# Four chunks of x in two loads, and one weight-block sum ordered behind four evictions, in a two-layer kernel with an order planned ahead

## The chip, the cores and the metric

The kernel runs on one core of a Trainium2 chip. The metric is the time of one execution on the device, in microseconds (us), of which the median of the runs is given.

## The reference, cut to what matters

There are 8 batches of 256 rows of x with 1024 features each, all in float32. Two layers follow each other, each with a residual. The first one's weights are a fixed matrix plus a sign matrix of the batch's own (an integer mask of zeros and ones), scaled by the batch's coefficient. The second one's weights are one of 8 matrices, chosen by the batch's index.

```python
output = jnp.einsum('bsi,oi->bso', hidden_states, W) + b
sign = (2 * mask - 1).astype(hidden_states.dtype)
diff = jnp.einsum('bsi,bio->bso', hidden_states, sign)
return output + diff * coeff[:, None, None]
...
w = weight[adapter_ids]
return jnp.einsum('bsi,boi->bso', x, w)
...
x = x + _L0_cond_ref(x, L0_cond_W, L0_cond_b, condB_coeff, mask_Bx4096x4096_ik1)
x = x + _L1_cond_ref(x, L1_cond_weight, itok_B_3_7)
```

## The kernel before, in words

**Stages.** There are 16 stages, (layer, batch): (0,0), (1,0), (0,1), (0,2), (1,1), (0,3), (1,2) and so on to (1,7) (L233). The first stage is made alone, in plain matmuls; each other stage is one product of x (256 rows) with a weight matrix of 1024 by 1024, cut in blocks of two by two ("11", "12", "21", "22"), and made by Strassen's scheme in Winograd's form: seven half-size products p1 to p7 in place of eight (L22), in the order p1, p5, p6, p2, p7, p3, p4 (L31). Each product is 16 matmuls in float32, each of which stands as two records in the profile.

**The first stage.** Its contraction of 1024 is made in 8 chunks of 128 rows. For chunks 0 to 2 the loads of a chunk's mask and weights come in two halves, for chunks 3 to 7 in one piece, so that there are 11 pieces, numbered n = 0 to 10; pieces 7, 8, 9 and 10 are the chunks 4, 5, 6 and 7. For each piece the mask comes by DMA, ScalarE turns it into a scaled sign (L307), VectorE adds the weights w0T ("fold", L315) and TensorE multiplies (L322). Mask and weights go out on SyncE's DMA queue (SP) in turns, the mask first but for piece 0 (L280 to L295). x of the first batch, transposed, goes out on the same queue between them (L275): chunk 0 behind the mask of piece 0, chunk 1 behind the weights of piece 1, chunks 2 and 3 behind the weights of piece 3, and chunks 4 to 7 together (x0d, 512 KB) behind the mask of piece 7. The last two chunks are multiplied in halves of the output: chunk 6 and chunk 7 of the first half, then both of the second half (L390). Four evictions add x and the bias and write the result, transposed, for the next stage: L349, two after the first half of the output, two after the second. They are the tasks collected in yT[0][1], which the second stage knows as `got`.

**The second stage**, (1,0), takes that transposed result with the operands of the matmul exchanged ("flipped", L602). Its weight blocks come as w1T by DMA, in the order 11, 12, 22, 21 (L528). VectorE makes the sums of weight blocks t1 = 12 - 11 (in two halves in this stage), t2 = 22 - t1, t3 = 22 - 12 and t4 = 21 - t2 (L568), and the sums of x blocks s1 to s4 (L551). p1 needs block 11 and the first two evictions; p5 needs s1 and t1, and s1 needs all four evictions; p6 needs s2 and t2; p7 needs s3 and t3; p4 needs t4. The products gather in three PSUM banks; copies by ScalarE (L653) and additions by VectorE (L681) read them out between products, and the next product into a bank waits for that.

**The stages after.** For layer 0 the mask blocks come by DMA (L515), ScalarE scales them (L524) and VectorE folds the weights in (L538). x comes as rows (xR, L417) and transposed (xT, L492), and the bias is added by a DMA of GpSimd's queue (L427). A result of layer 0 is turned for layer 1 by transposes on VectorE (L448) and 32 moves on ScalarE (L462).

**What sets the order.** A planner (L83) simulates all tasks with fixed lengths (a product 3.435, a block sum or fold 2.21, a small VectorE operation 0.61, a load 2.50 apart and 2.2 to land; L47) and writes each engine's order out, which is then the program's order[...]. Of the tasks that are ready, an engine takes the one with the earliest due time (`latest`), which is counted back from a timetable of the products: the second stage begins at 34.5, and each product is 3.435 after the one before. Blocks of weights, loaded or summed, stand in 11 buffers; t1 (of the second stage), t2 and t3 take a fresh one. A load waits for its buffer on the SP queue, and all loads behind it wait too.

In the second stage the three sums are asked for in these lines; the list in brackets says what they wait for besides their operands:

```python
if s == 1:
    sum_of("t1")
    sum_of("t2", got)
    sum_of("t3")
else:
    sum_of("t3")
    sum_of("t1", [done["t3"]])
    sum_of("t2")
```

Of the kernel before, what the change touches and what calls it, by code (L numbers as in the profile page):

```python
# [14 lines left out]
P = 128  # L15
# [127 lines left out]
def kernel(  # L143
# [9 lines left out]
    x0b: bass.AP,  # L153
    x0c: bass.AP,
    x0d: bass.AP,
    mask0: bass.AP,
    bias: bass.AP,
    biasT: bass.AP,
# [64 lines left out]
    def task(*args, **kw):  # L223
        tasks.append(Task(*args, **kw))
        return tasks[-1]

    def take(r: Buffer):
        count[0] += 1
        r.tile = pools[r.pool].tile(shapes[r.pool], F32, tag=r.pool, name=f"{r.pool}_{count[0]}")
        return r.tile  # L230
# [28 lines left out]
    x0 = Buffer("a")  # L259
# [11 lines left out]
    def m_view(k: int):  # L271
        flat = m[k // 2].tile.rearrange("p k n -> p (k n)")
        return flat.rearrange("p (k n) -> p k n", k=2)[:, k % 2]

    def load_x0(lo: int, source):  # L275
        size = source.shape[1] - PAD
        flat = x0.tile.rearrange("p q k n -> p (q k n)")
        nc.sync.dma_start(out=flat[:, ds(lo * 2 * TH, size)], in_=source[:, 0:size])  # L278

    def load_first(n: int, what: str):  # L280
        k, cols = pieces[n]
        if what == "mask":
            if m[k // 2].tile is None:
                take(m[k // 2])
            nc.sync.dma_start(out=m_view(k)[:, cols].bitcast(I32), in_=mask0[k][:, cols])  # L285
        elif n == 0:
            nc.sync.dma_start(out=w0_sb[:, 0 : B + cols.size], in_=w0T[0][:, 0 : B + cols.size])  # L287
        else:
            nc.sync.dma_start(
                out=w0_rows[:, k, cols], in_=w0T[k][:, ds(B + cols.start, cols.size)]  # L290
            )
        if what == "w" and n in (1, 3):
            load_x0(*{1: (1, x0b), 3: (2, x0c)}[n])
        if what == "mask" and n in (0, 7):
            load_x0(*{0: (0, x0a), 7: (4, x0d)}[n])  # L295

    def parts(n: int):

# [60 lines left out]
    for n, (k, cols) in enumerate(pieces):  # L359
        share = cols.size / D  # L360
        opens = opened != k // 2
        length = {0: 0.4, 6: 0.75}.get(n, 1.22 * share)

        loads_ = {}
        for what in ("w", "mask") if n == 0 else ("mask", "w"):
            takes = [m[k // 2]] if opens and what == "mask" else []
            loads_[what] = task(
                "DMA",
                1.32 * share,
                lambda n=n, what=what: load_first(n, what),  # L370
                takes=takes,
                uses=[] if takes or what == "w" else [m[k // 2]],
                latency=1.5,
                latest=0.2 * n + 0.1 * len(loads_),
            )
        ld, ld2 = loads_["mask"], loads_["w"]
        sc = task("ACT", length, lambda n=n: scale_first(n), after=[ld], uses=[m[k // 2]])
        fo = task("DVE", length, lambda n=n: fold_first(n), after=[sc, ld2], uses=[m[k // 2]])
        folded.append(fo)
        last_scale = sc  # L380
        opened = k // 2
        if n == 0:
            first_w = ld2
            ld.takes = [x0, *ld.takes]
            ld.uses = [x0, *ld.uses]
            x0.users += 1
# [91 lines left out]
    def stage(s: int):  # L478
# [7 lines left out]
        if layer == 0:  # L486
            A = Buffer("a")
            got = [
                task(
                    "DMA",  # L490
                    LOAD,
                    lambda: nc.sync.dma_start(out=take(A)[:, 0:4], in_=xT[b - 1]),  # L492
                    takes=[A],
                    latency=LATENCY,
                    earliest=begin - 7 * PRODUCT,
                )
            ]
        else:
            A, got = yT[b]
# [4 lines left out]
        def part(name: str):  # L504
            if flipped and name == "s3":
                return (apart.tile if apart.tile is not None else take(apart))[:, 0].rearrange(
                    "p (k n) -> p k n", k=KH
                )
            return A.tile[:, A_SLOT[name]]
# [35 lines left out]
        def sum_of(what: str, after=()):  # L545
            left, op, right = SUMS[what]
            if what[0] == "s":
                done[what] = task(
                    "DVE",
                    SMALL,  # L550
                    lambda: v.tensor_tensor(part(what), part(left), part(right), op),  # L551
                    after=[*got, done.get(left), done.get(right), *after],
                    takes=[apart] if flipped and what == "s3" else [],
                    uses=[A],
                )
                return
            src = [W[left], W[right]]
            fresh = what in ("t2", "t3") or (what == "t1" and s == 1)
            W[what] = Buffer("w") if fresh else W[left]

            parts = (slice(0, KH),)
            if s == 1 and what == "t1":
                parts = (slice(0, KH // 2), slice(KH // 2, KH))

            def emit(rows):
                a, c = src[0].tile[:, rows], src[1].tile[:, rows]
                to = W[what].tile if W[what].tile is not None else take(W[what])
                v.tensor_tensor(to[:, rows], a, c, op)  # L568

            for n, rows in enumerate(parts):  # L570
                t = task(
                    "DVE",
                    BLOCK / len(parts),
                    lambda rows=rows: emit(rows),
                    after=[done[left], done[right], done.get(what), *after],
                    takes=[W[what]] if fresh and n == 0 else [],
                    uses=src + ([W[what]] if fresh and n else []),
                )
                if fresh and n == 0:
                    t.stage = s  # L580
                done[what] = t
# [3 lines left out]
        if s == 1:  # L585
            sum_of("t1")
            sum_of("t2", got)
            sum_of("t3")
        else:
            sum_of("t3")  # L590
            sum_of("t1", [done["t3"]])
            sum_of("t2")
# [208 lines left out]
    for s in range(1, len(stages)):  # L801
        stage(s)
# [87 lines left out]
```

## Time and profile before

| what | value |
|---|---|
| median of 3 runs | 403.43 us (403.40 to 403.67) |
| the profiled execution's own time | 403.51 us |
| its span, first to last instruction | 401.8 us |
| TensorE busy (matmul) | 395.2 us |
| VectorE busy | 331.0 us |
| ScalarE busy | 184.4 us |
| granted TensorE clock | 1.000 |
| moved by DMA | 103.00 MB |

The profile names TensorE's matmuls PE, its weight loads PEld, VectorE DVE, ScalarE ACT, GpSimd POOL and SyncE's queue SP. A line of the timeline reads: start, duration (both in us), engine, source line, operation, written tile, read tiles, shapes, number of instructions merged in it, and in brackets the idle time of the engine ahead of it and what ended that. A line of the chain reads: start, duration, what. The row of digits for an engine or for DMA gives its busy share, in tenths, in each of 40 equal slices of the span (here of some 10 us each).

### The profile page before, as it was taken

What the parts mean: (1) busy time and instruction counts of PE and PEld (TensorE: products, weight loads), DVE (VectorE), ACT (ScalarE), POOL (GpSimd) and SP (SyncE); (2) the same over time, 40 slices, a digit from 0 to 9 for tenths busy, and PEclk for the clock granted to TensorE, in tenths of its full rate; (3) what the DMA queues carried; (4) which work ended last, traced back from release to release, by engine and by line L of the source; (5) the groups of instructions that cost most, each with busy time, mean ns of one, the idle gap of its engine ahead of it and who ended that gap; (6) DMA issues with size and microseconds to landing.
All of it is one profiled execution on the core that took longest, in us unless ns stands there. A gap on an engine that the chain in (4) does not pass through costs nothing.

```text
span 401.8 us, 3439 instructions
## 1 busy us (share of the span) xinstructions
PE 395.2 (98%) x1155; PEld 200.6 (50%) x1155; DVE 331.0 (82%) x307; ACT 184.4 (46%) x305; POOL 27.2 (7%) x44
## 2 busy tenths in 40 slices
PE   8999999999999999999999999999999999999996
PEld 4878995444444444444444444444444444444443
DVE  2347999999999999799968998789977999668142
ACT  4452635205952396880069600894109920291000
POOL 0100111100011100011010100101001020001101
PEclk9999999999999999999999999999999999999999
DMA  7999999993696829958399583997749694611102
GB/s 261 406 413 423 420 341 394 370 320 107 254 346 194 354 104 343 335 161 325 106 407 301 185 333 107 377 263 261 262 188 347 198 359 164 263 51 52 54 0 105
DMA packets 19154, 103.00 MB, mean 256 GB/s; under 512 B 2304, under 2 KB 2816, under 8 KB 9664
## 3 DMA queue, kind: packets, MB, share of 16 engines
q1 hardware_dynamic: 14544, 87.24, 56.3%
q0 software_dynamic: 4448, 15.47, 14.3%
q8 instruction: 9, 0.15, 0.1%
q10 hardware_dynamic: 144, 0.07, 0.1%
q14 instruction: 9, 0.07, 0.0%
HBM read 94.38 MB, written 8.39 MB: 256 GB/s over the span
## 4 chain that ended last, share of the span: by engine, by line
PE 89%; DMA 8%; issue 1%; DVE 1%; SPq 0%; DVEq 0%
PE ps L617 84%; PE ps L607 5%; DMA w<-w1T 4%; DMA w_sb<-w0T 2%; DMA w<-mask 2%; DVE a L349 0%; SPq L285 0%; DVE a L551 0%; SPq L278 0%; SPq L287 0%; DVE r L766 0%; DVE w L568 0%; DVEq L349 0%
## 5 line engine op out<-in xcount | busy, mean ns | idle before, releaser
L617 PE MATMUL ps<-w,a 128*128 128x512 f32 (+1 forms) x792 | 336.7, 588 | 0.0
L617 PEld LDWEIGHTS ps<-w,a 128*128 128x128 f32 x792 | 149.9, 190 | 186.7 <-issue 183.4
L568 DVE TENSOR_TENSOR w<-w,w 128x2048 f32<-128x2048 f32 (+1 forms) x61 | 136.9, 2252 | 3.8 <-PE ps L617 2.5
L462 ACT ACTIVATE a<-turn 32x256 f32<-32x256 f32 x224 | 92.8, 414 | 68.5 <-DVE turn L448 65.6
L681 DVE TENSOR_TENSOR r<-r,ps 128x512 f32<-128x512 f32 x73 | 49.0, 679 | 24.9 <-PE ps L617 24.6
L538 DVE TENSOR_TENSOR w<-w,w_sb 128x2048 f32<-128x2048 f32 x28 | 63.9, 2284 | 5.7 <-ACT w L524 5.7
L524 ACT ACTIVATE w<-w,cn_sb,c_sb 128x2048 f32<-128x2048 int32 x28 | 58.5, 2091 | 17.0 <-DMA w<-mask 16.7
L551 DVE TENSOR_TENSOR a<-a 128x512 f32<-128x512 f32 x59 | 39.4, 684 | 0.3
L653 ACT ACTIVATE s<-ps 128x512 f32<-128x512 f32 x15 | 8.9, 591 | 61.3 <-PE ps L617 53.9
L322 PE MATMUL ps<-a,w 128*128 128x256 f32 x128 | 28.9, 384 | 1.1 <-DVE w L315 1.1
L707 POOL DMA_DIRECT2D out<-r x31 | 17.0, 550 | 190.5 <-DVE r L681 190.4
L322 PEld LDWEIGHTS ps<-a,w 128*128 128x128 f32 x128 | 24.0, 192 | 6.1 <-DVE w L315 2.7
L653 ACT ACTIVATE u<-ps 128x512 f32<-128x512 f32 x15 | 8.9, 594 | 38.9 <-PE ps L617 38.8
L315 DVE TENSOR_TENSOR w<-w,w_sb 128x512 f32<-128x512 f32 (+2 forms) x13 | 10.5, 815 | 15.6 <-ACT w L307 8.7
L607 PE MATMUL ps<-a,w 128*128 128x128 f32 x192 | 22.0, 276 | 1.2 <-DVE a L551 1.2
L607 PEld LDWEIGHTS ps<-a,w 128*128 128x128 f32 x192 | 21.8, 192 | 1.5 <-DVE a L551 1.4
L448 DVE STREAM_TRANSPOSE turn<-r 128x512 f32<-128x512 f32 x28 | 19.7, 707 | 0.6
L427 POOL DMA_DIRECT2D r<-bias x7 | 8.7, 1245 | 169.1 <-DMA r<-xR 169.1
L307 ACT ACTIVATE w<-w,cn_sb,c_sb 128x512 f32<-128x512 int32 (+2 forms) x13 | 11.6, 909 | 14.7 <-DMA w<-mask 14.7
L681 DVE TENSOR_TENSOR r<-r,s 128x512 f32<-128x512 f32 x14 | 9.6, 684 | 6.6 <-ACT s L653 6.6
L681 DVE TENSOR_TENSOR r<-r,u 128x512 f32<-128x512 f32 x14 | 9.6, 685 | 3.4 <-ACT u L653 3.4
L812 PE MATMUL idle<-zeros 128*128 128x512 bf16 (+1 forms) x11 | 4.4, 593 | 1.2 <-DVE warm L807 1.2
(24 smaller groups left out, 23.1 us busy)
## 6 DMA issues: line engine op xcount, KB each, us to landing
w<-w1T SPq DMA_DIRECT2D x32, 1024.0 KB, 9.1
w<-mask SPq DMA_DIRECT2D x28, 1024.0 KB, 9.6
out<-r POOLq DMA_DIRECT2D x31, 256.0 KB, 7.3
r<-xR SPq DMA_DIRECT2D x7, 1024.0 KB, 6.8
a<-xT SPq DMA_DIRECT2D x7, 1024.0 KB, 6.9
r<-bias POOLq DMA_DIRECT2D x7, 1024.0 KB, 15.8
w<-mask SPq DMA_DIRECT2D x5, 512.0 KB, 9.1
w_sb<-w0T SPq DMA_DIRECT2D x5, 512.0 KB, 9.7
```

What stands on the lines that cost most here:

```text
L322: nc.tensor.matmul(out=t.rearrange("p (c n) -> p c n", c=half)[:, c % half], lhsT=m_view(k)[:, ts(oc, P)], rhs=x0_view()[:, k], start=k == ...
L448: lambda t=t, opens=not turned: v.transpose(out=(take(r) if opens else r.tile)[:, t], in_=view(source.tile)[:, 2 * t + j]),
L462: nc.scalar.activation(to[:, :, :, f], src[:, :, :, g], AF.Copy)
L524: nc.scalar.activation(t, t.bitcast(I32), AF.Identity, bias=cn_sb[:, b : b + 1], scale=c2_sb[:, b : b + 1])
L538: lambda q=q: v.tensor_tensor(W[q].tile, W[q].tile, w0[q], ALU.add),
L551: lambda: v.tensor_tensor(part(what), part(left), part(right), op),
L568: v.tensor_tensor(to[:, rows], a, c, op)
L607: nc.tensor.matmul(out=t[:, ts(c, TH)], lhsT=W[w].tile[:, k, ts(c, P)], rhs=part(a)[:, k], start=opens and c == 0 and k == 0, stop=k == KH ...
L617: nc.tensor.matmul(out=t[:, cols], lhsT=part(a)[:, k], rhs=W[w].tile[:, k, cols], start=opens and k == 0, stop=k == KH - 1, skip_group_che ...
L653: lambda: nc.scalar.activation(take(r), bank.tile, AF.Copy),
L681: v.tensor_tensor(to, left, get(r), op)
L707: lambda: (queue or nc.gpsimd).dma_start(out=out0[:, block(q)] if flipped else out[b - 1, :, int(q[0]) - 1, lo:hi], in_=R[b].tile[:, block ...
```

## The change

The loads of x for the first batch: x0d now holds chunks 4 and 5 alone (256 KB) and stays behind the mask of piece 7; a new array x0e holds chunks 6 and 7 (256 KB) and goes out behind the mask of piece 9, which is chunk 6. In the second stage, t3 gets the four evictions of the first stage as predecessors, as t2 had already. The rest of the diff passes the new array on. The lengths and the due times that the planner works with are not changed.

```diff
-        if what == "mask" and n in (0, 7):
-            load_x0(*{0: (0, x0a), 7: (4, x0d)}[n])
+        if what == "mask" and n in (0, 7, 9):
+            load_x0(*{0: (0, x0a), 7: (4, x0d), 9: (6, x0e)}[n])
...
         if s == 1:
             sum_of("t1")
             sum_of("t2", got)
-            sum_of("t3")
+            sum_of("t3", got)
...
-    for k, chunks in (("x0a", x0[:, 0]), ("x0b", x0[:, 1]), ("x0c", x0[:, 2:4]), ("x0d", x0[:, 4:8])):
-        arrays[k] = chunks.reshape(P, -1)
+    for k, lo, hi in (("x0a", 0, 1), ("x0b", 1, 2), ("x0c", 2, 4), ("x0d", 4, 6), ("x0e", 6, 8)):
+        arrays[k] = x0[:, lo:hi].reshape(P, -1)
...
-    for k in ("x0a", "x0b", "x0c", "x0d", "w0T", "mask0"):
+    for k in ("x0a", "x0b", "x0c", "x0d", "x0e", "w0T", "mask0"):
```

More of the change, by code (lines that the diff above doesn't have):

```diff
@@ L155 @@
     x0d: bass.AP,
+    x0e: bass.AP,
     mask0: bass.AP,
```

## The prediction

> **What bounds the kernel now.** I read the page's busy line first, then the chain that ended last, then the timelines of the stretch that the change touches.
>
> ```profile
> PE 395.2 (98%) x1155; PEld 200.6 (50%) x1155; DVE 331.0 (82%) x307; ACT 184.4 (46%) x305; POOL 27.2 (7%) x44
> DMA 7999999993696829958399583997749694611102
> PE 89%; DMA 8%; issue 1%; DVE 1%; SPq 0%; DVEq 0%
> ```
>
> TensorE is the bound nearly throughout; the DMA engines are full for the first nine slices (90 us). The 8% of DMA on the chain lie at its start, as the chain in order of time shows:
>
> ```profile
> 12.43 9.09 DMA w<-mask
> 21.54 14.64 DMA w<-w1T
> 36.20 0.03 DVE w L568
> ...
> 38.41 1.29 DVE a L349 x2
> 39.70 0.02 issue
> 39.73 0.70 DVE a L551
> 40.43 0.04 issue
> 40.48 21.70 PE ps L607 x192
> 62.18 336.52 PE ps L617 x792
> ```
>
> From 40.48 us on TensorE never stops. So whatever starts that row earlier is the kernel's gain, as long as no operand comes late afterwards. Ahead of it, the chain passes through a weight block landing at 36.18, a block sum (L568), two evictions and s1. The timelines of TensorE and VectorE show the stalls:
>
> ```profile
> 20.34 1.23 DVE L315 TENSOR_TENSOR w<-w,w_sb 128x1024 f32<-128x1024 f32 x1 [2.56 <-DMA w_sb<-w0T]
> 21.61 14.08 PE L322 MATMUL ps<-a,w 128*128 128x256 f32 x64 [0.66 <-DVE w L315]
> 28.82 1.23 DVE L315 TENSOR_TENSOR w<-w,w_sb 128x1024 f32<-128x1024 f32 x1 [2.13 <-ACT w L307]
> 33.78 4.71 DVE L568 TENSOR_TENSOR w<-w,w 128x1024 f32<-128x1024 f32 x3 [0.74 <-DMA w<-w1T]
> 38.41 1.28 DVE L349 TENSOR_TENSOR a<-ps,r 128x512 f32<-128x512 f32 x2
> 40.48 10.98 PE L607 MATMUL ps<-a,w 128*128 128x128 f32 x96 [1.21 <-DVE a L551]
> ```
>
> Two stalls concern us. At 20.95 TensorE waits 0.66 us for chunk 4's fold, itself waiting for chunk 4's w0T. At 39.26 it waits 1.21 us for s1: the first stage's matmuls end at 35.69, but its last two evictions stand behind t3 (third of the x3) on VectorE and start at 38.41.
>
> **What the Trainium skill says.** "PSUM — Partial Sum Buffer", Engine vs sequencer instructions: VectorE's queue is strict FIFO. The trace agrees: the evictions' data was there 2.7 us before they ran. "DMA: Bandwidth & Descriptors", Queues, rings and completion order: each engine takes descriptors in ring order. The trace agrees: issue plus time to landing gives 19.0 for x0d, 20.3 for chunk 4's w0T, and so on in issue order, 0.65 us per 256 KB, 1.28 per 512 KB and 2.48 per MB. "SBUF — State Buffer", The DMA setup-cost knee: about 2 us fixed cost per transfer. Here it doesn't show in the landing intervals, which are proportional to bytes even for 128 KB; the transfers overlap.
>
> **First edit: x0d split.** Removed: 256 KB ahead of chunk 4's w0T. Added: one issue on SP (0.33 us, the row of x0c) behind chunk 6's mask. Moved earlier by 0.65 us: w0T of chunk 4, both loads of chunk 5, the mask of chunk 6. From chunk 6's w0T on all bytes ahead are the same. x0e lands about 24.1 and is needed about 28.0. SP issues some 8 us ahead of landing, which covers its 0.33; a wait for an older DMA that moves by one place costs an issue up to 1.3 us, also covered.
> - Chunk 4: fold starts 19.7, ends 20.93, matmuls begin 20.98 in place of 21.61: 0.63 earlier.
> - Chunks 5 and 6 follow at 24.54 and 28.0; their folds end 23.5 and 26.7.
> - Chunk 7 is **what is late next**: its fold starts 28.82 when its w0T has landed (17.69 + 11.0 = 28.7), unchanged, and ends 30.05. Its matmuls began at 30.35, so only 0.3 us of the shift passes; the other 0.35 becomes a new stall there. A first product after a stall runs about 0.1 us slower (p5 to p6 took 3.67 against 3.575 for the later ones).
> I take 0.20 gained. Bounds: -0.1 (x0e's own handling, if nothing passes) and 0.63 (if chunk 7's data comes earlier too). First stage ends 35.5.
>
> **Second edit: t3 behind the evictions.** No instruction is added or removed; t3 waits for four evictions on the same engine. By the planner's own lengths and due times, worked by hand: when the evictions are done, s1 is due 37.3, t2 39.2, s2 40.8, the first eviction of p1 43.1, t3 46.0, p5's eviction 46.5, s3 47.6. So VectorE's order becomes t1, t1, evictions, s1, t2, s2, eviction 11, t3, eviction 22, s3, s4. In chip time, with 2.20 us per block operation and 0.60 per small one, back to back: t1 33.78 to 36.1 (still bound by block 12's landing, 20.26 + 13.4 = 33.7), evictions to 37.3, s1 done 38.0. p1 runs 35.3 to 38.9, so p5 no longer waits.
> - From p1's start to p6's start is now 44.15 - 35.53 = 8.62; two products at 3.575 are 7.15. **Gain 1.47** (1.21 idle plus the slower pace after it). Bounds: 1.21 and 1.47.
> - Behind t3's wait are queued eviction 22, s3 and s4: done 44.2, 44.8 and 45.4 against needs of 49.6 or later. t3 itself is done at 43.6; p7 wants it at 49.6.
> - Block 12's buffer and t3's change places in the order of release. Mask loads went out the moment p1, p5, p7, p3 ended (39.30, 44.34, 55.06, 58.64): they take buffers in order of release. t3 now takes an older, free buffer; the 44.34 load now waits for t3's end, 43.6 instead. Nothing on SP gets later.
>
> **What is late next.** VectorE is full from 33.8 to 130 (26.37 of 26.5 us, then 66.69 of 67.8), so TensorE can't simply move 1.67 us ahead; I checked each product's operands.
> - By the planner's clock the folds of the next masks now come ready together, and block 12's goes first: VectorE would be free at 45.3 but that fold waits for its ACT scaling, done 45.82. It is then 0.3 us later than before, up to the 0.91 us at 68.19 in which it waited for TensorE; that idle goes, and from 69.09 on it is about 0.68 earlier.
> - p4 of this stage needs p7's bank read. It started at 55.57; with one fold put ahead of it and 0.3 us of lateness it starts 55.88 and ends 56.57, against p4's start at 58.44 - 1.67 = 56.77. Close.
> - p6 of the next stage needs the ACT copy behind the scaling at 63.75: 66.3 against 67.2.
> - Product p1 of batch 1's second layer needs 32 ACT moves, which follow VectorE's transposes:
>
> ```profile
> 93.50 1.30 DVE L448 STREAM_TRANSPOSE turn<-r 128x512 f32<-128x512 f32 x2
> 98.45 10.63 ACT L462 ACTIVATE a<-turn 32x256 f32<-32x256 f32 x25
> ```
>
> They ended 1.01 us ahead of need (109.08 against 110.09). 1.01 + 0.68 - 1.67 = 0.02: just enough, and a cap near 1.7 on the whole gain. After 130 us VectorE waits for TensorE in every stage, so it moves along.
>
> **Sum.** 0.20 + 1.47 = 1.67, given back 0 (0 to 0.5). Profiled execution: 403.51 (span 401.8 plus 1.71 around it) - 1.67 = 401.84. The median of the runs shown is 0.08 lower: 401.8.
>
> **Rivals.**
> A. As above, 401.4 to 402.3: chance 0.64.
> B. VectorE becomes the bound: TensorE keeps little more than VectorE's own advance of 0.7 to 1.0, the rest comes back as small stalls at p4 or at the ACT moves. About 402.5. For: VectorE at 99% over 95 us and margins of 0.2 and 0.02 us; against: both are still positive. 0.18, of it 0.15 below 402.6.
> C. A block fold of 2.20 us goes ahead of p7's bank read in that stage: p4 would start 58.77 in place of 56.77 and the gain is gone: 403.43 - 1.67 + 2.0 = 403.8. For: the planner puts one fold ahead already by a few hundredths; against: a second would be due later than that read. 0.10. That t3 stays ahead of the evictions is excluded, as its wait forbids it; that t2 (due 39.2) passes s1 (37.3) would leave 402.4 and belongs to B.
> D. Slower: the mask load issued at 44.34 now hangs on t3. If t3 sinks behind the folds to about 50, this load goes out 6 us later, SP's queue behind it too; it landed at 63.67, ACT's scaling follows, and the copy that p6 needs stands behind that. From 0.9 us later landing each microsecond stops TensorE; above 66.2 it outweighs the gain. Landing 4 us later costs 3.1: 404.9. Against: t3 is due before all folds. 0.05.
> (0.03 are left for more than 1.9 us gained.)
>
> **Numbers.** Range 401.3 to 402.6: A whole, B's upper part to its middle, the first edit's upper bound cut by the cap. Measurement can tell about 0.2%, 0.8 us: faster means below 402.62. Faster 0.64 + 0.15 + 0.03 = 0.82; same 0.13; slower 0.05.
>
> **What would show it.** First edit: chunk 4's 0.66 stall below 0.1 and a new one of about 0.35 near 29.7. Second: evictions at 36.1, no stall at p5, p6's start at 42.5, t3 between the first two product evictions near 41.4. No stall of TensorE over 0.2 us after 62. A stall at p4 near 56.8 or ahead of p1 near 108.4 makes B; a mask landing after 64.6 makes D.

## The result, and the profile after

| | before | after |
|---|---|---|
| median of 8 runs each | 403.65 us | 402.14 us |
| range | 403.40 to 404.02 | 401.98 to 402.86 |
| profiled execution, its own time and span | 403.51, 401.8 | 402.02, 400.2 |

The ratio is 0.9965 with a 95% interval of 0.9955 to 0.9976: faster by 1.5 us, 0.35%. The prediction was 401.8 (401.3 to 402.6), and 1.67 us gained.

The shares of the chain, of the changed kernel's page:

```profile
PE 94%; DMA 4%; DVE 0%; SPq 0%; issue 0%; DVEq 0%
```

DMA's share of the chain has fallen from 8% to 4%. The chain in order of time (start, duration, what) shows where it went:

```profile
12.06 7.87 DMA w_sb<-w0T
...
20.03 1.24 DVE w L316
21.27 0.04 issue
21.31 14.20 PE ps L323 x64
35.51 25.01 PE ps L608 x224
60.52 336.52 PE ps L618 x792
```

Block 12's and 22's landing, t3 and the evictions are gone from it. From chunk 4's fold on, the chain is TensorE alone. (All lines of the source have moved by one: L618 is L617 of before.) The last 98 products take 336.52 us in both profiles; they start at 60.52 in place of 62.18, 1.66 us earlier.

The timelines of VectorE and TensorE, for the stretch of the change:

```profile
28.79 1.23 DVE L316 TENSOR_TENSOR w<-w,w_sb 128x1024 f32<-128x1024 f32 x1 [1.74 <-DMA w_sb<-w0T]
33.75 2.36 DVE L569 TENSOR_TENSOR w<-w,w 128x1024 f32<-128x1024 f32 x2 [0.89 <-DMA w<-w1T]
36.03 1.28 DVE L350 TENSOR_TENSOR a<-ps,r 128x512 f32<-128x512 f32 x2
37.34 0.69 DVE L552 TENSOR_TENSOR a<-a 128x512 f32<-128x512 f32 x1
41.36 2.28 DVE L569 TENSOR_TENSOR w<-w,w 128x2048 f32<-128x2048 f32 x1
45.81 4.49 DVE L539 TENSOR_TENSOR w<-w,w_sb 128x2048 f32<-128x2048 f32 x2 [0.36 <-ACT w L525]
55.82 0.68 DVE L682 TENSOR_TENSOR r<-r,ps 128x512 f32<-128x512 f32 x1
...
35.35 14.46 PE L608 MATMUL ps<-a,w 128*128 128x128 f32 x128
```

The x3 of before has become the x2 of t1; the evictions follow at 36.03, s1 at 37.34, and t3 is the lone block sum at 41.36. TensorE runs four products from 35.35 without a break, where it stood 1.21 us ahead of p5. p7's bank read (55.82) ends at 56.50, and p4 starts at 56.79.

### The profile page after: what moved, and what is told of

Read it like the earlier page. It is cut to its first block, busy times and chain, and to the rows that moved or that the text cites. A ratio compares the mean times of both kernels' runs of the same rounds, so it can differ in the third digit from the quotient of the medians.

```text
span 400.2 us, 3444 instructions
## 1 busy us (share of the span) xinstructions
PE 394.2 (98%) x1155; PEld 200.0 (50%) x1155; DVE 330.6 (83%) x307; ACT 184.2 (46%) x305; POOL 27.2 (7%) x44
## 4 chain that ended last, share of the span: by engine, by line
PE 94%; DMA 4%; DVE 0%; SPq 0%; issue 0%; DVEq 0%
PE ps L618 84%; PE ps L608 6%; PE ps L323 4%; DMA w<-mask 2%; DMA w_sb<-w0T 2%; DVE w L316 0%; SPq L279 0%; SPq L286 0%; SPq L288 0%; DVE r L767 0%; DVEq L316 0%
## 5 line engine op out<-in xcount | busy, mean ns | idle before, releaser
L618 PE MATMUL ps<-w,a 128*128 128x512 f32 (+1 forms) x792 | 336.7, 588 | 0.0
L618 PEld LDWEIGHTS ps<-w,a 128*128 128x128 f32 x792 | 149.9, 190 | 186.7 <-issue 182.7
```

The source lines that it names most:

```text
L618: nc.tensor.matmul(out=t[:, cols], lhsT=part(a)[:, k], rhs=W[w].tile[:, k, cols], start=opens and k == 0, stop=k == KH - 1, skip_group_che ...
```

## The experiments

Eleven runs were made, two of them of the changed kernel itself, each beside the kernel before on the same chip, with 4 to 22 executions each. The ratios are estimates with intervals and not the quotients of the two medians beside them. They stand in three groups, each on its own chip: the rows beside 403.61; the third time and the two kernels with x later; and the other four. "p1" is the start of the second stage's first product in the profiled execution.

| kernel | median | of before beside it | ratio, 95% interval | p1 |
|---|---|---|---|---|
| x0d split alone | 404.01 | 403.79 | 1.0006 (0.9999 to 1.0012) | 35.66 |
| t3's place alone | 402.30 | 403.79 | 0.9966 (0.9954 to 0.9978) | 35.54 |
| changed kernel again | 402.08 | 403.79 | 0.9960 (0.9947 to 0.9973) | 35.53 |
| changed kernel, third time | 402.35 | 403.79 | 0.9967 (0.9954 to 0.9979) | 35.26 |
| chunk 7's fold in halves | 402.31 | 403.79 | 0.9964 (0.9952 to 0.9976) | 35.44 |
| t3 longer | 403.10 | 403.61 | 0.9986 (0.9978 to 0.9995) | 35.58 |
| block 11's fold first | 402.14 | 403.61 | 0.9963 (0.9949 to 0.9976) | 35.13 |
| one load late | 402.18 | 403.61 | 0.9960 (0.9945 to 0.9976) | 35.76 |
| halves and block 11 first | 401.97 | 403.61 | 0.9964 (0.9950 to 0.9978) | 35.09 |
| that, and x later still | 401.87 | 403.79 | 0.9948 (0.9935 to 0.9961) | 35.22 |
| halves, x later, block 12 first | 402.07 | 403.79 | 0.9957 (0.9944 to 0.9970) | 35.56 |

The theory was the prediction's: the gain is the new place of t3; the split adds a little, up to what chunk 7's weights allow; behind that, margins of VectorE and ScalarE of a few tenths of a microsecond cap it.

**The parts one by one.** First the split alone:

```diff
-            sum_of("t3", got)
+            sum_of("t3")
```

> The split of x0d alone, t3 put back ahead of the evictions. Theory of the prediction: no gain, 0.0 us against before (-0.15 to +0.1). The first stage ends about 0.2 us earlier (p1 starts near 35.3), but its last two evictions still stand behind t3, which starts when block 12 and 22 have landed and t1 is done, so that s1 ends at 40.4 and p5 starts at 40.4 to 40.5 as before; the idle time ahead of p5 grows from 1.21 to about 1.4 us. Rival, in which the two edits simply add up: -0.2 us, p5 0.2 us earlier. Rival, in which relieving the DMA queue ahead of chunk 4 is the change's real worth: -0.6 us or more.

Measured: 1.0006, no gain. Its timeline of TensorE:

```profile
30.38 5.45 PE L323 MATMUL ps<-a,w 128*128 128x256 f32 x24 [0.56 <-DVE w L316]
35.66 3.73 PE L608 MATMUL ps<-a,w 128*128 128x128 f32 x32
40.76 10.98 PE L608 MATMUL ps<-a,w 128*128 128x128 f32 x96 [1.36 <-DVE a L552]
```

The stall ahead of p5 stands, 1.36 us (1.21 before). But the first stage didn't end earlier either: chunk 7's matmuls (30.38) waited 0.56 us for their fold, though chunk 4's had begun at 20.50, 1.1 us earlier than before. So the cover by t3 is not the only reason for nothing gained.

Then t3's place alone, the kernel before with

```diff
-            sum_of("t3")
+            sum_of("t3", got)
```

> The new place of t3 alone, x0d in one load as before. Theory: -1.47 us against before (-1.2 to -1.6): p1 starts at 35.5, p5 follows without idle time near 39.1, p6 starts near 42.7, and the shift of about 1.45 us stays to the end; chunk 4's stall of 0.6 to 0.7 us near 21 is there as before. Rival, in which the split is the main part: -0.6 us or less. Rival, in which VectorE takes the shift back in the next two stages: under -1.0 us, with idle time of TensorE between 56 and 110 us.

Measured: 0.9966, 402.30, which is the whole change's gain within the intervals. TensorE's timeline:

```profile
21.62 14.08 PE L322 MATMUL ps<-a,w 128*128 128x256 f32 x64 [0.67 <-DVE w L315]
35.54 14.46 PE L607 MATMUL ps<-a,w 128*128 128x128 f32 x128
```

Chunk 4's stall of 0.67 is there, the one ahead of p5 is not. It decides between the edits: nearly all of the gain is the order of VectorE.

**The changed kernel twice more**, unedited, since the first runs reached from 401.98 to 402.86.

> The changed kernel once more, beside the others on the same chip. Theory: -1.6 us against before (-1.4 to -1.75), p1 at 35.3, p6 at 42.5, no idle time of TensorE over 0.2 us after that. Rival, in which small stalls of VectorE or ScalarE come in some executions since the margins are 0.15 to 0.6 us: -1.0 to -1.3.

> The changed kernel a third time, beside the two on the same chip: -1.5 us against before (-1.2 to -1.7), with p1 at 35.3 to 35.6 and single stalls under 0.5 us at p7 or p4 of the second stage in some executions.

The medians are 402.08 and 402.35. The profiled execution of the second time was slower than the first one's, 400.9 us of span against 400.2, and shows a stall that the prediction had not listed. ScalarE and TensorE in it:

```profile
47.56 2.10 ACT L525 ACTIVATE w<-w,cn_sb,c_sb 128x2048 f32<-128x2048 int32 x1 [1.58 <-DMA w<-mask]
49.56 0.57 ACT L654 ACTIVATE u<-ps 128x512 f32<-128x512 f32 x1
...
50.19 3.84 PE L608 MATMUL ps<-turn,w 128*128 128x128 f32 x32 [0.20 <-ACT u L654]
```

and ScalarE in the first profile of the changed kernel:

```profile
46.16 2.10 ACT L525 ACTIVATE w<-w,cn_sb,c_sb 128x2048 f32<-128x2048 int32 x1 [0.39 <-DMA w<-mask]
48.16 0.58 ACT L654 ACTIVATE u<-ps 128x512 f32<-128x512 f32 x1
```

A mask block landed 1.4 us later (47.47 against 46.08), its scaling followed, and the copy that p7 waits for stood behind the scaling on ScalarE. p7 had a margin of 2.51 us before the change and 0.90 after it, and lost 0.47 us here: from p2's start to p7's 3.95 in place of 3.575, and 0.1 in the product after, which ran slower. The rival of small stalls was right for this execution; the median, 1.71 us below that of before, lies in the theory's range.

**What bounds the first stage.** The changed kernel with chunk 7's scaling and fold (piece 10) in two halves:

```diff
-        size = {0: 2 * P, 6: H}.get(n, cols.size)
+        size = {0: 2 * P, 6: H, 10: H}.get(n, cols.size)
```

> The changed kernel, with the scaling and the fold of chunk 7 of the first stage in two halves of 512 columns, so that its first matmuls wait for half of the fold only. Theory (chunk 7's weights, landing at 28.7, are what comes late next in the first stage): the first half of the fold ends near 29.5 in place of 30.0, the step from chunk 6's first half to chunk 7's falls to TensorE's own 1.73 us and the slower product after it goes; p1 starts 0.1 to 0.3 us earlier than in the changed kernel, depending on how early the first chunks came in that execution. Of it the whole kernel keeps 0.1 to 0.15, since the ACT moves ahead of p1 of batch 1's second layer were done only 0.15 us ahead of need; in all -1.7 us against before. Rival, in which TensorE's own pace sets the end of the first stage already: the same time as the changed kernel, -1.6.

Measured: 0.9964, no difference to the changed kernel; p1 at 35.44. In this execution chunk 7's weights landed late, at 29.29, and its matmuls followed at 30.16, 0.87 us behind. With the fold in one piece they follow the landing by 1.37 to 1.45 us in all seven profiles with the split (landing 28.47 to 29.10; here the landing is the issue plus its time to landing). In the two profiles without the split they follow by 1.63 and 1.82: there TensorE came later than the data. So the theory's mechanism holds, and what moves p1 between 35.1 and 35.8 is that landing.

The landing is then the point to count from. The table does so for the profiles of all runs, one execution each:

| first stage | profiles | landing of chunk 7's weights | p1 behind it |
|---|---|---|---|
| x0d in one load | before, t3's place alone | 28.72, 28.54 | 6.81, 7.00 |
| split, fold in one piece | seven | 28.47 to 29.10 | 6.65 to 6.66 |
| split, halves | halves; halves and block 11 first | 29.29, 28.79 | 6.15, 6.30 |
| halves, x later still | block 11 first; block 12 first | 29.07, 29.40 | 6.15, 6.15 |

So the halves do bring p1 forward, by 0.36 to 0.51 us behind the same landing. With the order of folds as in the changed kernel none of it is kept. VectorE's row of the second stage hangs on the same landing: block 12 lands 4.96 to 4.98 us behind chunk 7's weights in all thirteen profiles, and t1 begins 5.06 to 5.08 us behind them. p7's bank read therefore does not come earlier with p1, and p4 waits for it:

```profile
53.31 7.70 PE L608 MATMUL ps<-a,w 128*128 128x128 f32 x64
```

These two products, p3 and p4, take 7.31 us in the changed kernel. The 0.39 lost here and 0.11 more ahead of p1 of batch 1's second layer, where ScalarE's moves end at 108.87 against a start at 108.92, take back 0.50 of the 0.51. The profiled execution's time less the landing is 373.27 us, against 373.33 and 373.31 in the changed kernel's first and third profiles. The theory had placed the limit at the moves alone.

More of x behind the weights was tried then: chunk 3 alone behind chunk 3's weights, chunks 4 and 5 behind chunk 4's, with the halves and block 11's fold first:

```diff
-        if what == "w" and n in (1, 3):
-            load_x0(*{1: (1, x0b), 3: (2, x0c)}[n])
-        if what == "mask" and n in (0, 7, 9):
-            load_x0(*{0: (0, x0a), 7: (4, x0d), 9: (6, x0e)}[n])
+        if what == "w" and n in (1, 3, 6, 7):
+            load_x0(*{1: (1, x0b), 3: (2, x0c), 6: (3, x0f), 7: (4, x0d)}[n])
+        if what == "mask" and n in (0, 9):
+            load_x0(*{0: (0, x0a), 9: (6, x0e)}[n])
```

> Fold of chunk 7 in halves, block 11's fold first, and x of the first batch later still on the queue: chunk 3 alone behind the weights of chunk 3, chunks 4 and 5 behind the weights of chunk 4. Theory (what precedes a load in bytes is what it waits for, 0.65 us per 256 KB, until chunk 7's w0T at 28.7 bounds): the matmuls of chunk 3 start near 17.2, those of chunk 4 near 20.7, those of chunk 7 near 29.5, p1 near 34.7 to 34.8. That is 0.35 us ahead of the same kernel without these moves and 0.6 to 0.8 ahead of the changed kernel; the wider margins (0.5 to 0.7 us) let nearly all of it through: -0.5 us against the changed kernel (-0.3 to -0.7), -2.1 against before. Rival, in which the last weights' landing fixes the end of the first stage whatever stands ahead: -0.2 against the changed kernel.

Measured: 0.9948, 401.87, the best of all kernels tried, though its interval overlaps that of the changed kernel. Chunk 4 began at 20.53, as foretold, but p1 at 35.22 and not 34.7. VectorE's folds of chunks 6 and 7, and TensorE:

```profile
26.61 1.23 DVE L317 TENSOR_TENSOR w<-w,w_sb 128x1024 f32<-128x1024 f32 x1 [3.05 <-DMA w_sb<-w0T]
29.19 1.29 DVE L317 TENSOR_TENSOR w<-w,w_sb 128x512 f32<-128x512 f32 x2 [1.35 <-DMA w_sb<-w0T]
...
27.89 7.49 PE L324 MATMUL ps<-a,w 128*128 128x256 f32 x32 [0.29 <-DVE w L317]
```

What was gained at chunk 4 turned into waits for the weights of chunks 6 and 7. Chunk 7's weights landed at 29.07, 0.4 us later than the theory had taken, which makes most of the difference at p1. Behind that landing p1 stands at 6.15, where the halves without these moves had it at 6.15 and 6.30. On the mechanism the rival was right: once the halves are in, the landing of the last weights fixes the end of the first stage, and what stands ahead adds 0.15 us at most. The time does not decide between the two sizes: 401.87 is 0.48 below the changed kernel on the same chip (402.35) and 0.21 below its lowest median.

**The margins.** First VectorE's: t3's first quarter computed twice more, unknown to the planner, so that no order changes.

```diff
                 v.tensor_tensor(to[:, rows], a, c, op)
+                if s == 1 and what == "t3":
+                    for _ in range(2):
+                        v.tensor_tensor(to[:, 0:1], a[:, 0:1], c[:, 0:1], op)
```

> The changed kernel with VectorE made to compute the first quarter of t3 twice more (two added operations of 0.60 us, the same values; the planner does not know of them, so that no order changes). It measures VectorE's margin. Theory: of 1.2 us, 0.36 to 0.45 vanish in VectorE's wait for the scaling of block 12; 0.8 us pass on. p4 of the second stage had 0.28 us to spare and starts 0.5 us later; the ACT moves ahead of p1 of batch 1's second layer had 0.15 and cost 0.1 to 0.2 more. In all +0.6 us against the changed kernel (+0.4 to +0.8), -1.0 against before. Rival, in which TensorE is the one bound and VectorE has room: 0. Rival, in which VectorE is the bound outright: +1.2.

Measured: 403.10, 0.96 us more than the changed kernel's 402.14, which was timed beside a kernel before of 403.65 where this one had 403.61. VectorE and TensorE:

```profile
43.91 1.42 DVE L572 TENSOR_TENSOR w<-w,w 128x512 f32<-128x512 f32 x2
45.24 0.68 DVE L685 TENSOR_TENSOR r<-a,ps 128x512 f32<-128x512 f32 x1
...
47.05 4.49 DVE L539 TENSOR_TENSOR w<-w,w_sb 128x2048 f32<-128x2048 f32 x2
57.05 0.68 DVE L685 TENSOR_TENSOR r<-r,ps 128x512 f32<-128x512 f32 x1
...
57.79 3.84 PE L611 MATMUL ps<-a,w 128*128 128x128 f32 x32 [0.61 <-DVE r L685]
```

From t3's start to the next addition it is 3.65 us in place of 2.20 (41.59 to 45.24, against 41.36 to 43.56): the two operations cost 1.45, not 1.2. 0.45 of it vanished in the wait ahead of the folds, 0.28 in p4's margin; that leaves 0.72, and p4 started 4.35 us after p3 in place of 3.575, 0.78 late. It ran 0.10 slower after its stall, and ahead of p1 of batch 1's second layer, where the moves ended at 109.50 against a start at 109.55, another 0.12 was lost. That is 1.00 in all, for the 0.96 measured. The mechanism and both places of loss were as expected, the size was not. VectorE has no room here: what it is late beyond p4's margin costs TensorE all of it.

Then block 11's fold first, which takes away VectorE's wait for the scaling:

```diff
-                    after=[t],
+                    after=[t, *([done["11"]] if s == 2 and q == "12" else [])],
```

> The changed kernel, with the fold of block 11 ahead of that of block 12 in the third stage, so that VectorE doesn't wait for block 12's scaling near 45.4. Theory: VectorE is some 0.4 us earlier from 48 on, the margins at p4 and ahead of p1 of batch 1's second layer grow from 0.28 and 0.15 to about 0.7 and 0.55, and the time stays that of the changed kernel (within 0.15 us), as TensorE had no stall left there. Rival, in which VectorE bounds the stages to 130 us: -0.4 us against the changed kernel.

Measured: 402.14, the changed kernel's time. The folds began at 45.14 right behind s4, p7's bank read ended at 55.97 against p4's start at 56.95, a margin of 0.98 in this execution. Of that, 0.28 is a stall at p7, as in the second time's profile: here too the mask block landed late, 3.60 us behind the load ahead of it, and the copy (49.07 to 49.65) came just ahead of p7, which started 3.85 us after p2:

```profile
49.70 3.84 PE L608 MATMUL ps<-turn,w 128*128 128x128 f32 x32
```

Without it the margin is 0.70, as foretold. The stall and the slower product after it cost this execution 0.38 us; its time less the landing is 373.67, 0.34 more than the changed kernel's first. A wider margin alone brings nothing, and it doesn't guard p7.

With the halves together:

> The changed kernel with chunk 7's fold in halves and the fold of block 11 ahead of that of block 12. Theory: what the halves bring to the end of the first stage (0.1 to 0.3 us) is kept whole, as the margins of VectorE and of the ACT moves are 0.4 us wider: -0.1 to -0.3 us against the changed kernel, -1.7 to -2.0 against before. Rival: nothing beyond the changed kernel.

Measured: 401.97, 0.1 to 0.4 below the three medians of the changed kernel; the intervals overlap. In the profile p1 stands 6.30 behind the landing, p4 has no stall, and the execution's time less the landing is 372.98, 0.35 below the changed kernel's 373.33. So the theory holds there, in one execution: what the halves bring is kept once VectorE is ahead. And the kernel with x later, but with block 12's fold first again, which was to show the cap on the gain:

> The same loads and halves, but with the fold of block 12 first, as in the changed kernel. It tries the cap on the gain. Theory: the first stage ends 0.6 to 0.8 us earlier than in the changed kernel, but p4 of the second stage had 0.28 us to spare and p1 of batch 1's second layer 0.15; so all but about 0.2 us comes back as stalls of TensorE at these two places: -0.2 us against the changed kernel (-0.1 to -0.3), 0.3 behind the kernel with block 11 first. Rival, in which there is no such cap: the same as the kernel with block 11 first.

Measured: 402.07 against 401.87 with block 11 first; the intervals overlap. p1 came at 35.56 only because chunk 7's weights landed at 29.40; behind that landing it stands at 6.15, as with block 11 first. TensorE's line has the stall at p4, as products p3 and p4 take 7.70 us in place of 7.31:

```profile
53.42 7.70 PE L609 MATMUL ps<-a,w 128*128 128x128 f32 x64
```

Ahead of p1 of batch 1's second layer 0.12 more is lost (moves to 108.99, start at 109.05). The execution's time less the landing is 373.31, as in the changed kernel, against 372.80 with block 11 first. So the cap is there: in this profile the whole 0.5 us came back at the two places named. Between the medians the difference is 0.20.

**The load that hangs on t3.** The prediction's slower case, tried directly: a small transfer that waits for the fold of block 11, ahead of the mask load of the fourth stage's block 12.

```diff
+            if (s, q) == (3, "12"):
+                nc.sync.dma_start(out=late, in_=folded_11[0].tile[0:1, 0, 0:8])
             t = take(W[q])
```

> The changed kernel, with one small transfer (32 bytes between two places of SBUF) put on the SP queue ahead of the mask load of block 12 of the fourth stage, which waits for VectorE's fold of block 11 (done 50.2), so that this load goes out near 50.7 in place of 43.7. It tries the prediction's case D directly. Theory: the load's turn in the DMA rings comes after the landing of the one ahead of it (58.8), so that it lands at 64.0 as before, within 0.3 us, and the time stays that of the changed kernel within 0.2 us. Rival (case D): a load that goes out 7 us later lands up to 7 us later, the scaling and the copy that p6 needs follow, and TensorE loses all but 0.6 us of it: +3 to +6 us.

Measured: 402.18, no difference. SP's queue and ScalarE in this kernel:

```profile
50.74 0.81 SPq L517 DMA_DIRECT2D late<-w  x1
51.61 2.27 SPq L520 DMA_DIRECT2D w<-mask  x2
...
64.28 2.09 ACT L529 ACTIVATE w<-w,cn_sb,c_sb 128x2048 f32<-128x2048 int32 x1 [3.11 <-DMA w<-mask]
```

The load went out at 51.61, 7.9 us later than in the changed kernel (43.67), and its scaling began at 64.28 against 64.08, in an execution whose second stage was 0.41 us late as a whole. It landed at 64.19 against 63.99: the loads ahead of it on the queue set its landing, not its issue. For a delay of this size the case falls.

## Why the prediction was right, and where its sizes were off

**The second edit, 1.47.** Right, in mechanism and size: from p1's start to p6's it was 8.62 us and is 7.14 (35.35 to 42.49), 1.48 less. t3's place alone gives 403.79 - 402.30 = 1.49. The order worked out from the planner's due times was the order on the chip, operation by operation in that stretch; evictions at 36.03, s1 done at 38.03 and t3 at 43.64 were foretold as 36.1, 38.0 and 43.6.

**The first edit, 0.20.** Right in mechanism, and lost in the scatter. From chunk 3's start to chunk 4's it was 4.38 us and is 3.79, 0.59 less where 0.63 was worked out, and chunk 7 was late next, as said. The stall of 0.35 foretold there was not in the first profile, in which chunk 3 began 0.29 us later than before and chunk 7's matmuls right behind their fold (30.07, the fold's end 30.02). Three others with the split (the split alone, t3 longer, one load late) have it, with 0.56, 0.24 and 0.54. Behind the same landing p1 comes 0.15 us earlier than in the kernel before (6.66 against 6.81) and 0.34 earlier than with t3's place alone (7.00), on both sides of the 0.20. But the step took that landing as the fixed 28.7 of one execution, and it scatters from 28.47 to 29.10, more than the 0.20 in question. Over the seven profiles with the split and the fold in one piece, p1 starts at 35.47 in the mean (35.13 to 35.76), against 35.53 and 35.54 without it. In time no gain can be seen. The split alone gained nothing, as t3 covers it there; the end of the execution is some 0.1 us longer with it (see the sum below); and the changed kernel's three medians lie from 0.22 below to 0.05 above that of t3's place alone.

**What is late next.** All three margins were of the size foretold: p4 0.28 (foretold 0.20), the copy ahead of p6 0.57 (0.9), the ACT moves ahead of p1 of batch 1's second layer 0.15 (0.02). The last is read in ScalarE's timeline of the changed kernel, the moves ending at 108.28 against a start at 108.43:

```profile
97.65 10.63 ACT L463 ACTIVATE a<-turn 32x256 f32<-32x256 f32 x25
```

The list was not complete: the copy ahead of p7, with 0.90 left of 2.51, was missing, and it gave way in two of the eleven profiles with t3 behind the evictions, once in the changed kernel and once with block 11's fold first. The margin at p4 is the firmer limit: it is 0.27 to 0.28 in the three profiles that have the split, the folds in this order and no stall, though the landing went from 28.60 to 29.10, since p1 and VectorE's row move together with it.

**Given back, 0 (0 to 0.5).** 0 in the first profile. In the second time's profile TensorE was 1.48 us ahead of before at p6 of the second stage and 1.01 ahead at the start of the last stage: 0.47 given back, at p7.

**The rivals.** B came in single executions of the changed kernel and not as the rule; where the first stage was made to end earlier with the folds in the planner's order, it held in both profiles. C had its one fold ahead and no second one. D was tried and fell.

**The sum.** 1.67 foretold. TensorE's last 98 products start 1.66 earlier. That this fits to 0.01 is luck: 0.18 of it is p1's place in that one execution (35.35 against 35.53), and p1 scattered over 0.63 us in the seven profiles. The profiled executions differ by 1.49 (403.51 to 402.02) and the medians by 1.51. The missing 0.15 lies behind the last product: from the last addition's end to the span's end it is 2.88 us (397.36 to 400.24) in place of 2.74 (399.01 to 401.75). That end is 2.74 and 2.75 in the two profiles without the split and 2.83 to 2.95 in all eleven with it; the last store lands 1.69 and 1.70 us behind the last addition there and 1.86 to 1.96 here. So it goes with the split, for which the prediction had no such term, and its cause is open. The rest to 401.8 is the kernel before, whose median was 403.65 over eight runs and not the 403.43 of the three shown.

## What to carry to other kernels

On an engine that works in order, look for what stands ahead of the instruction that the bounding engine waits for, and ask when the one ahead is needed: t3 was wanted 12.8 us after it was made, and cost 1.5 us by its place alone. A stall removed at the start is worth only what the next operand's margin allows, so list each product's margin before counting the gain, all of them. A load moved back on a full queue helps what comes between its old and new place and nothing behind it; the end of the stage comes earlier only until the last load's landing sets it. And where one landing scatters by more than an edit is worth, count the profiles' times from that landing: here the changed kernel's three lie 0.27 us apart at p1 as they stand, and agree to 0.01 counted so.

## What the runs showed that was not expected

Single transfers land late though the queue is full and its order fixed. In all thirteen profiles one load of the first stage's last three is 0.3 to 1.5 us late, and everything behind it moves along; this is a part of the scatter of chunk 7's landing. In each of them one packet of the instruction queue (16 KB, on one DMA engine, 1.1 us) falls shortly before, at 24.1 to 25.5 us. Where it came at 24.05 to 24.61, the late load was chunk 6's weights; at 24.74 to 25.30, chunk 7's mask; at 25.45, chunk 7's weights. One case: in the kernel before, chunk 7's mask landed 2.09 us after the load ahead of it in place of 1.28.

A second such packet falls at 44.7 to 47.5 us. There a load was late by more than 0.1 us in seven profiles of thirteen, by 0.15 to 1.2 us. In two of them it was the mask block that p7's copy depends on, 3.68 and 3.60 us in place of 2.48 behind the load ahead: these are the two with the stall at p7. In the second time's profile the stretch from 43.8 to 47.6 holds these packets (queue, then the number of packets, MB, and their share of the 16 engines' time):

```profile
q1 hardware_dynamic: 220, 1.56, 99.2%
q8 instruction: 1, 0.02, 1.8%
```

The second packet came at 47.0 and 47.5 in the two profiles with the stall ahead of p5, and at 44.7 to 45.6 in all others, so it moves with the program. It is not enough by itself: it came at 45.33 and 44.84 in the two profiles with the late mask block, and at 45.41 and 44.71 in two where no load was late. That the packets are the cause, at either place, was not tried.
